# Layer 1: values projected once a pixel and moved to the patch positions by transfers within SBUF

## The chip, the cores and the metric

The kernel runs on one core of a Trainium2 chip. The metric is the device time of one execution in microseconds. Three runs of the kernel before gave 4286.24, 4290.92 and 4291.43 us; the median is 4290.92.

The engines are named as in the profile: PE (TensorE: matrix products; PEld is its loading of the stationary operand, which overlaps), DVE (VectorE), ACT (ScalarE), POOL (GpSimd), and SP (SyncE), which computes nothing and issues DMAs. SBUF is the working memory of 128 partitions, PSUM the memory that PE writes.

## The reference

The network has four layers, numbered 0 to 3, on images of 56 x 56 pixels with 192 channels, 8 in the batch, all in float32; each layer adds its result to its input after a group norm. The change is in layer 1, the second one, an attention over 3 x 3 patches with stride 2:

```python
v = x @ Wv
vp = jnp.pad(v, ((0, 0), (PAD, PAD), (PAD, PAD), (0, 0)))
patches = jnp.stack([vp[:, i:i + STRIDE * h:STRIDE, j:j + STRIDE * w:STRIDE, :] for i in range(K) for j in range(K)], axis=3)
patches = patches.reshape(Bn, h * w, KK, HEADS, HEAD_DIM)
pooled = x.reshape(Bn, h, STRIDE, w, STRIDE, C).mean(axis=(2, 4))
a = pooled.reshape(Bn, h * w, C) @ Wa + ba
a = a.reshape(Bn, h * w, HEADS, KK, KK) * SCALE
a = jax.nn.softmax(a, axis=-1)
out = jnp.einsum('bnhpq,bnqhd->bnphd', a, patches)
...
for i in range(K):
    for j in range(K):
        acc = acc.at[:, i:i + STRIDE * h:STRIDE, j:j + STRIDE * w:STRIDE, :].add(out[:, :, :, idx, :])
        idx += 1
...
return y @ Wp + bp
```

There are 28 x 28 positions an image and 9 places in each patch (K is 3, KK is 9), so a pixel stands in 9/4 patches in the mean. The value of a pixel, `x @ Wv`, doesn't depend on the patch in which it stands. There are 6 heads of 32 channels.

## The kernel before, in words

Layer 1 works on units, `(p, t)`: a pair of images p (4 of them) and a strip t of 8 image rows (7 of them), 28 units in all. Channels lie on partitions: parts j = 0 and 1 hold the first 128 channels of the two images, part 2 the other 64 channels of both, one image on partitions 0 to 63, the other on 64 to 127 (`sides`).

For unit n the steps are:

- `load(n)` issues 6 DMAs for the strip (L788).
- `normalize(n)` has ACT scale and shift the strip into `xn` (L834), where rows stand in pairs and each has a column of zeros ahead of it (57 columns, `W1`). One more pair of rows at the top holds the row above the strip, copied from the unit before or cleared (L829, L831). POOL adds 2 x 2 pixels into `pool` (L839, L841).
- `patches(n)` copies `xn` nine times, once for each place q in the patch, into `xc`, so that for each position the nine pixels stand side by side: five copies on DVE, two on POOL (q 3 and 7), two on ACT (q 1 and 5) (L856 to L860).
- `values` multiplies `xc` by `Wv`. A step takes one row of 28 positions, as two groups of 14 positions x 9 places = 126 pixels, for two images: eight matmuls (L924, L930), with the pixels stationary and the 192 columns of `Wv` moving, and one eviction on ACT (L934). There are four steps in a unit. The result, `v`, has (q, position) on 126 partitions.
- `attention` has two parts. `logits` multiplies `pool` by `Wa` (L875, L879), adds the bias and subtracts the largest (DVE, POOL). `weights` takes the exponential (ACT), sums and inverts (DVE), scales (POOL, L895) and stores the result to DRAM as `ad` (L900).
- `spread` brings `ad` back into `bd` with 14 DMAs (L913), in such a layout that the matrix `bd` of a group has its attention weights in the right columns and zeros elsewhere. There are two `bd` buffers.
- `attend` multiplies `v` by `bd` (L959): 96 matmuls, 8 groups of 12, whose sums in PSUM are at once the weighted sum and the adding back to the image. It evicts to `ys` and carries the row that two strips share.
- `fold` multiplies `ys` by `Wp` (L1002 to L1013) and adds the result to the strip (L1025). `finish` stores it with 6 DMAs (L984) and takes statistics for the next layer's norm.

The loop over units n (L1064) is a pipeline written out by hand. In one turn it loads unit n + 4, normalizes n + 3, makes the patches of n + 2, attends n, multiplies the logits of n + 2, makes the values of n + 1 (with the weights of n + 2 after the second step), spreads n + 2 and folds n. Ahead of the loop units 0 and 1 are brought to the same state.

The order of PE, DVE, ACT and POOL is the program's (`manual_schedule` at L770). SP is not in that list: the order of its DMAs is set by the framework's planner when the program is built. [...]

Most DMAs of the kernel, and all of layer 1's loop, are issued on SP. Two buffers `c` in PSUM serve logits, values and fold in turn.

Of the kernel before, what the change touches and what calls it, by code (L numbers as in the profile page):

```python
# [10 lines left out]
ALU = mybir.AluOpType  # L11
# [4 lines left out]
C = 192  # L16
CP = 96
H = 56
# [712 lines left out]
def layer1(cx, xin, xout, w, consts):  # L731
# [27 lines left out]
    with ExitStack() as es:  # L759
# [55 lines left out]
        nc.sync.dma_start(bp, w["bp"])  # L815

        xns = [cx.tile(cp, [128, NR + 1, 3, 2, W1], f"xn{i}") for i in range(2)]


        bds = [cx.tile(cp, [NP, 2 * NG, NCOL, HEADS, 3], f"bd{i}") for i in range(2)]
# [1 line left out]
        def normalize(n):  # L824

            p, t = units[n]
            x, xn = xs[n], xns[n % 2]
            if t == 0:
                nc.gpsimd.memset(xn[:, 0, :, 1, :], 0.0)  # L829
            else:  # L830
                nc.gpsimd.tensor_copy(xn[:, 0, :, 1, :], xns[(n - 1) % 2][:, NR, :, 1, :])  # L831
            for j in range(3):
                s, o = norms[p][:, j, 0:1], norms[p][:, j, 1:2]
                nc.scalar.activation(  # L834
                    xn[:, 1:, j, :, 1:], x[:, j].rearrange("p (y i x) -> p y i x", i=2, x=H),
                    AF.Identity, bias=o, scale=s,
                )
            rows = cx.tile(sp, [128, NR, 3, H], "rows")
            nc.gpsimd.tensor_tensor(rows, xn[:, 1:, :, 0, 1:], xn[:, 1:, :, 1, 1:], ALU.add)  # L839
            pool4 = cx.tile(wk, [128, 3, NR, N], "pool")  # L840
            nc.gpsimd.tensor_tensor(  # L841
                pool4.rearrange("p j y x -> p y j x"), rows[:, :, :, 0:H:2], rows[:, :, :, 1:H:2], ALU.add
            )
            return pool4.rearrange("p j y x -> p j (y x)")

        def patches(n):

            xn = xns[n % 2]
            xc = cx.tile(wk, [128, 3 * NR, 2, KK, NX], "xc")
            for q in range(KK):  # L850
                j, i = divmod(q, 3)
                src = xn[:, (i + 1) // 2 : (i + 1) // 2 + NR, :, (i + 1) % 2, j : j + 2 * N - 1 : 2]
                src = src.rearrange("p y j (u x) -> p (y j) u x", u=2)
                dst = xc[:, :, :, q, :]
                if q in (3, 7):
                    nc.gpsimd.tensor_copy(dst, src)  # L856
                elif q in (1, 5):
                    nc.scalar.copy(dst, src)
                else:
                    nc.vector.tensor_copy(dst, src)  # L860
            return xc

        def attention(pool4, out):

# [47 lines left out]
                at = 2 * x * 3 * HEADS  # L912
                nc.sync.dma_start(bd[x : x + (KK - 1) * NX + 1 : NX, :, at : at + HK], av[x])  # L913

        def values(xc, v):


            def step(r):
                pv = cx.tile(psc, [128, 2, 512], "c")
                out = lambda i, u: pv[0:NP, i, u * C : (u + 1) * C]  # L920
                group = lambda j, u: xc[:, 3 * r + j, u].rearrange("p q x -> p (q x)")
                for u in range(2):
                    for i in range(2):
                        nc.tensor.matmul(  # L924
                            out(i, u), group(i, u), wv[0], start=(u == 0), stop=True,
                            skip_group_check=True,
                        )
                for u in range(2):
                    for i in range(2):
                        nc.tensor.matmul(  # L930
                            out(i, u), group(2, u)[sides[i]], wv[1][sides[i]], start=False, stop=True,
                            skip_group_check=True,
                        )
                nc.scalar.copy(  # L934
                    v[:, :, 2 * r : 2 * r + 2, :].rearrange("p i g c -> p i (g c)"),
                    pv[0:NP, :, 0 : 2 * C],
                )

            return [lambda r=r: step(r) for r in range(NR)]


        blocks = [[(0, h) for h in range(4)], [(1, h) for h in range(4)]]
# [3 lines left out]
        def attend(n, v):  # L946
# [4 lines left out]
            for g in range(NG):  # L951
                r, half = divmod(g, 2)
                i0 = int(t == 0 and r == 0)
                c0 = int(half == 0)
                dims = (NCOL - c0, 3 - i0)
                to = (half * 2 * NX + c0 - 1) * NY + 2 * r + i0
                for k, block in enumerate(blocks):
                    for u, (i, h) in enumerate(block):
                        nc.tensor.matmul(  # L959
                            sub(py[u * HD : (u + 1) * HD, k, to:], (NY, dims[0]), (1, dims[1])),  # L960
                            v[:, i, g, h * HD : (h + 1) * HD],
                            bd[:, i * NG + g, c0:, h, i0:],
                            start=(g == 0), stop=True, skip_group_check=True,
                        )
# [68 lines left out]
        def clear(n):  # L1033
            (nc.gpsimd, nc.vector)[n].memset(bds[n], 0.0)

        vs, xcs, pools = {}, {}, {}
        for i, xn in enumerate(xns):
            nc.gpsimd.memset(xn[:, :, :, :, 0], 0.0)
        pools[0] = normalize(0)
        xcs[0] = patches(0)  # L1040
# [3 lines left out]
        first[0]()  # L1044
        pools[1] = normalize(1)
        clear(0)
        vs[0] = cx.tile(wk, [NP, 2, NG, C], "v")
        todo = values(xcs.pop(0), vs[0])
        todo.pop(0)()
        todo.pop(0)()  # L1050
        first[1]()
        spread(0, ads.pop())
        for f in todo:
            f()
        second = attention(pools.pop(1), ads)
        second[0]()
        clear(1)
        second[1]()
        spread(1, ads.pop())
        xcs[1] = patches(1)  # L1060
        pools[2] = normalize(2)
        for p in range(1, NPAIR - 1):
            fetch_norms(p, nc.sync)
        for n in range(len(units)):  # L1064
            if n == 2:
                for f in cx.late:
                    f(lambda: cx.tile(psb, [128, 512], "b"))
                fetch_norms(NPAIR - 1, nc.sync)
            load(n + 4)
            if n + 3 < len(units):  # L1070
                pools[n + 3] = normalize(n + 3)
            if n + 2 < len(units):
                xcs[n + 2] = patches(n + 2)
            ys = attend(n, vs.pop(n))
            if n + 1 < len(units):
                vs[n + 1] = cx.tile(wk, [NP, 2, NG, C], "v")
                todo = values(xcs.pop(n + 1), vs[n + 1])
                if n + 2 < len(units):
                    logits, weights = attention(pools.pop(n + 2), ads)
                    logits()  # L1080
                    todo.insert(2, weights)
                for f in todo:
                    f()
                if ads:
                    spread(n + 2, ads.pop())
            if late and late[0][0] <= n:
                late.pop(0)[1]()
            fold(n, ys)
# [950 lines left out]
```

## Time and profile before

| what | us |
|---|---|
| median of three runs | 4290.92 |
| the profiled execution | 4297.32 |
| its span, first to last instruction | 4295.5 |
| PE busy in the span | 4052.9 |
| DVE, ACT, POOL busy | 2340.9, 1781.9, 1510.6 |
| `attend` (L959), start of the first and the last matmul | 2150.6, 2753.5 |

The profile is one execution, taken by the hardware profiler. A row of a group names line, engine, operation, what is written and read, the number of instructions and their times. A row of a DMA issue (SPq) gives the time that the issue took on SP, not that of the transfer. "Busy" leaves DMA issues out. In a timeline, neighbouring instructions of one line are merged; its columns are start, duration, engine, line, operation and number. In the chain of waits, which is followed back from the last instruction, each piece is what the next one waited for. A window's columns are explained where one is shown. Some of PE's records are missing, so their numbers can be a few per cent low; each float32 matmul leaves two records.

### The profile page before, as it was taken

The numbers are of one execution on the slowest core, as the hardware profiler recorded it, in microseconds if no ns is written. First come the engines' busy times: TensorE is split into PE (matmuls) and PEld (weight loads), VectorE is DVE, ScalarE is ACT, GpSimd is POOL, SyncE is SP. The second block draws the span as 40 slices with busy tenths as digits, with TensorE's granted clock in tenths as the row PEclk, the third lists the DMA queues.
The fourth block names the chain that finished last, engine by engine and source line by source line (L and its number), as shares of the span: only waits on it lengthen the run. The fifth ranks groups of instructions, "written<-read, shape, count | busy, mean of one in ns | idle before, by whom it ended". The sixth has DMA issues, their size and how long they took to land.

```text
span 4295.5 us, 106533 instructions
## 1 busy us (share of the span) xinstructions
PE 4052.9 (94%) x46380; PEld 2655.7 (62%) x46380; DVE 2340.9 (54%) x3429; ACT 1781.9 (41%) x2052; POOL 1510.6 (35%) x1295
## 2 busy tenths in 40 slices
PE   6999999999999999999699999769998999998997
PEld 4666767676676767667366666524444555555997
DVE  4446565554656545554444444366665666664664
ACT  2334434334443333443233344223334555554664
POOL 3223232222322222232133333133334444444776
PEclk9999999999999999999899999889999999999999
DMA  6755242242524224241224344455547676664243
GB/s 137 143 106 144 61 114 62 78 96 61 143 62 111 56 74 109 61 109 59 80 72 109 96 107 105 121 173 171 165 140 180 171 174 156 155 152 114 71 117 93
DMA packets 379607, 484.14 MB, mean 113 GB/s; under 512 B 175780, under 2 KB 324372, under 8 KB 377236
## 3 DMA queue, kind: packets, MB, share of 16 engines
q1 hardware_dynamic: 373636, 466.97, 42.8%
q10 hardware_dynamic: 5504, 10.35, 0.8%
q8 instruction: 365, 5.98, 0.6%
q14 instruction: 102, 0.84, 0.1%
HBM read 321.49 MB, written 155.65 MB: 111 GB/s over the span
## 4 chain that ended last, share of the span: by engine, by line
PE 79%; DVE 6%; issue 5%; SPq 3%; DMA 3%; ACT 2%; POOL 1%; DVEq 0%; ACTq 0%; POOLq 0%
PE c L294 10%; PE c L376 6%; PE v L1371 6%; PE c L301 5%; PE c L462 4%; PE c L417 4%; PE c L924 4%; PE h L1873 4%; PE c L352 4%; PE y L959 3%; PE kv L1431 3%; PE c L442 3%; PE c L424 3%; DVE ol L359 2%; PE c L1583 2%
## 5 line engine op out<-in xcount | busy, mean ns | idle before, releaser
L325 POOL TENSOR_TENSOR qv<-s,s 128x392 f32<-128x392 f32 (+3 forms) x320 | 568.5, 1798 | 1453.5 <-ACT s L310 1453.0
L310 ACT ACTIVATE s<-c,bqv 128x784 f32<-128x784 f32 (+1 forms) x320 | 278.2, 910 | 383.9 <-PE c L301 189.1
L294 PE MATMUL c<-xa,wqv 128*128 128x392 f32 x1152 | 433.2, 518 | 4.3 <-DVE xa L49 2.7
L359 ACT COPY or<-c 56x1024 f32<-56x1024 f32 (+1 forms) x288 | 256.2, 901 | 424.4 <-DVE ol L359 414.5
L319 DVE TENSOR_TENSOR qv<-s,s 128x784 f32<-128x784 f32 (+1 forms) x160 | 205.8, 1287 | 265.0 <-ACT s L310 265.0
L359 DVE COPY ol<-c 56x1024 f32<-56x1024 f32 (+1 forms) x288 | 299.8, 1076 | 39.8 <-PE c L352 38.5
L294 PEld LDWEIGHTS c<-xa,wqv 128*128 128x128 f32 x1152 | 211.1, 194 | 176.8 <-issue 39.3
L376 PEld LDWEIGHTS c<-or,ol 120*64 120x64 f32 x9216 | 275.8, 139 | 39.5 <-issue 29.6
L376 PE MATMUL c<-or,ol 120*64 120x56 f32 x9216 | 284.5, 223 | 11.5 <-DMA ol<-ed 7.7
L352 PEld LDWEIGHTS c<-ident,qv 64*120 64x120 f32 x4032 | 256.1, 138 | 55.1 <-issue 35.6
L352 PE MATMUL c<-ident,qv 64*120 64x64 f32 x4032 | 282.8, 224 | 3.6 <-POOL qv L325 2.5
L1371 PE MATMUL v<-wvb,wa 128*128 128x512 f32 (+1 forms) x400 | 192.1, 612 | 50.5 <-ACT wa L1282 31.3
L301 PE MATMUL c<-xb,wqv 64*128 64x392 f32 x1152 | 232.9, 518 | 0.0
L431 ACT ACTIVATE s<-c,bp 128x448 f32<-128x448 f32 x224 | 129.7, 630 | 248.7 <-PE c L424 248.6
L1904 POOL TENSOR_TENSOR y<-y,s 128x448 f32<-128x448 f32 x168 | 185.0, 1101 | 92.7 <-ACT s L1883 92.7
L1873 PE MATMUL h<-ringv,am 128*64 128x57 f32 (+1 forms) x4400 | 192.7, 235 | 19.6 <-DVE ringv L1860 11.8
L462 PE MATMUL c<-po,wo 128*128 128x448 f32 x448 | 198.1, 564 | 7.0 <-DVE po L451 7.0
L1873 PE MATMUL h<-ringh,am 128*64 128x57 f32 (+1 forms) x4400 | 186.3, 232 | 7.8 <-DVE ringh L1879 7.8
L1382 ACT ACTIVATE vb<-sm 128x1024 f32<-128x1024 f32 (+1 forms) x100 | 103.7, 1038 | 212.2 <-issue 187.2
L417 PE MATMUL c<-xa,wp 128*128 128x224 f32 x896 | 191.1, 356 | 0.0
L405 DVE TENSOR_TENSOR acca<-c,acca 128x392 f32<-128x392 f32 (+1 forms) x120 | 67.3, 587 | 219.2 <-PE c L467 204.8
L1873 PEld LDWEIGHTS h<-ringv,am 128*64 128x64 f32 x4400 | 168.1, 140 | 22.9 <-DVE ringv L1860 12.7
(221 smaller groups left out, 7591.9 us busy)
## 6 DMA issues: line engine op xcount, KB each, us to landing
or<-tt SPq DMA_DIRECT2D x252, 196.0 KB
ol<-tt SPq DMA_DIRECT2D x252, 196.0 KB
vt<-v SPq DMA_DIRECT2D x56, 672.0 KB
v<-vb SPq DMA_DIRECT2D x96, 384.0 KB
x<-x SPq DMA_DIRECT2D x112, 168.0 KB
x<-x SPq DMA_DIRECT2D x112, 112.0 KB
bt<-bs SPq DMA_DIRECT2D x28, 448.0 KB
bs<-bs SPq DMA_DIRECT2D x56, 224.0 KB
```

What stands on the lines that cost most here:

```text
L294: nc.tensor.matmul(ps[:, h, 0:n], wqv[0][:, j, :], xn[0][:, at : at + n], start=True, stop=False,)
L301: nc.tensor.matmul(ps[:, h, 0:n], wqv[1][rows, j, :], xn[1][rows, g * n : (g + 1) * n], start=False, stop=True,)
L310: nc.scalar.activation(t, ps[rows, :, 0:n], AF.Silu, bias=bqv[rows, j : j + 1])
L319: nc.vector.tensor_tensor(sub(qv[rows, 7 * g :, 64 + H - 1 :], (HH * 120, 2), (120, 7), (-1, H)), *(t.rearrange("p u (h w) -> p u h w", w= ...
L325: eng.tensor_tensor(sub(qv[rows, w0:, H - 1 - 7 * g - HH * u :], (120, w1 - w0), (-1, 7)), *(t[:, u].rearrange("p (h w) -> p w h", w=H)[:, ...
L352: nc.tensor.transpose(view(i // 8)[:, :, i % 8], qv[e : e + DS, i0 + i, :], ident[e : e + DS, e : e + DS],)
L359: copy(dst, src[rows])
L376: nc.tensor.matmul(ps[u * 64 : (u + 1) * 64, k, v * H : (v + 1) * H], left[:, d * H : d * H + 64], right[:, d * H : (d + 1) * H], start=Tr ...
L417: nc.tensor.matmul(out(u, h), wp[0][:, 2 * j + u, :], xn[0][:, at : at + n], start=(u == 0), stop=True, skip_group_check=True,)
L462: nc.tensor.matmul(pa, wo[:, 2 * j + u, 0:CA], pos[u], start=(u == 0), stop=(u == 1))
L1371: nc.tensor.matmul(out, x[:, at : at + n], wt, start=(k == 0), stop=(k == 1), skip_group_check=True,)
L1873: nc.tensor.matmul(ps[sides[c], y], am[a][:, m * CB : (m + 1) * CB], old[:, x], start=(n < 2), stop=True, skip_group_check=True,)
```

## The change

- There is no `patches` and no `xc`. `xn` loses its extra pair of rows.
- `values(n)` multiplies each pixel of the strip once. A step takes two pairs of rows, 2 x 57 = 114 pixels each, for two images: eight matmuls as before, with 114 pixels stationary where there were 126. Two steps make a unit, each with one eviction on ACT. The result `vp` has (row of the pair, column) on 114 partitions and five pairs of rows; the first pair is the last one of the strip above, copied by POOL, or cleared at t = 0.
- `gather(n)` moves `vp` to `v`: for each of the nine places q and each half u of a row of positions, one DMA from every second of 27 partitions of `vp` to 14 partitions of `v`. Each is 14 x 4 x 384 numbers, in pieces of 1536 B: 18 DMAs a unit, 504 in all, on SP.
- There are three `v` buffers, not two, and the index of the image is now inside that of the group.
- In the loop, the values are made for unit n + 2, not n + 1, with the weights after the first step; then come the gather and the spread of n + 2.

```diff
-        xns = [cx.tile(cp, [128, NR + 1, 3, 2, W1], f"xn{i}") for i in range(2)]
+        xns = [cx.tile(cp, [128, NR, 3, 2, W1], f"xn{i}") for i in range(2)]
...
-            if t == 0:
-                nc.gpsimd.memset(xn[:, 0, :, 1, :], 0.0)
-            else:
-                nc.gpsimd.tensor_copy(xn[:, 0, :, 1, :], xns[(n - 1) % 2][:, NR, :, 1, :])
...
-        def patches(n):
-
-            xn = xns[n % 2]
-            xc = cx.tile(wk, [128, 3 * NR, 2, KK, NX], "xc")
-            for q in range(KK):
-                j, i = divmod(q, 3)
-                src = xn[:, (i + 1) // 2 : (i + 1) // 2 + NR, :, (i + 1) % 2, j : j + 2 * N - 1 : 2]
...
-        def values(xc, v):
+        def values(n):
+
+
+            xn = xns[n % 2]
+            vp = vps[n] = cx.tile(wk, [2 * W1, NR + 1, 2, C], "vp")
+            above = vps.pop(n - 1, None)
+            if units[n][1] == 0:
+                nc.gpsimd.memset(vp[:, 0], 0.0)
+            else:
+                nc.gpsimd.tensor_copy(vp[:, 0], above[:, NR])
...
-            def step(r):
+            def step(k):
                 pv = cx.tile(psc, [128, 2, 512], "c")
-                out = lambda i, u: pv[0:NP, i, u * C : (u + 1) * C]
-                group = lambda j, u: xc[:, 3 * r + j, u].rearrange("p q x -> p (q x)")
+                out = lambda i, u: pv[0 : 2 * W1, i, u * C : (u + 1) * C]
+                pixels = lambda j, u: xn[:, 2 * k + u, j].rearrange("p a x -> p (a x)")
...
-            return [lambda r=r: step(r) for r in range(NR)]
+            return [lambda k=k: step(k) for k in range(NR // 2)]
+
+        def gather(n):
+
+            rows = vs[n % NV].rearrange("p (r u) i c -> p u r (i c)", u=2)
+            for q in range(KK):
+                j, i = divmod(q, 3)
+                for u in range(2):
+                    at = (i + 1) % 2 * W1 + u * 2 * NX + j
+                    src = vps[n][at : at + 2 * NX - 1 : 2].rearrange("p r i c -> p r (i c)")
+                    r = int(i > 0)
+                    nc.sync.dma_start(rows[q * NX : (q + 1) * NX, u], src[:, r : r + NR])
...
+        NV = 3
+        vs = [cx.tile(cp, [NP, NG, 2, C], f"v{k}") for k in range(NV)]
+        vps, pools = {}, {}
...
+            ys = attend(n, vs[n % NV])
             if n + 2 < len(units):
-                xcs[n + 2] = patches(n + 2)
-            ys = attend(n, vs.pop(n))
-            if n + 1 < len(units):
-                vs[n + 1] = cx.tile(wk, [NP, 2, NG, C], "v")
-                todo = values(xcs.pop(n + 1), vs[n + 1])
-                if n + 2 < len(units):
-                    logits, weights = attention(pools.pop(n + 2), ads)
-                    logits()
-                    todo.insert(2, weights)
+                todo = values(n + 2)
+                logits, weights = attention(pools.pop(n + 2), ads)
+                logits()
+                todo.insert(1, weights)
                 for f in todo:
                     f()
-                if ads:
-                    spread(n + 2, ads.pop())
+                gather(n + 2)
+                spread(n + 2, ads.pop())
```

More of the change, by code (lines that the diff above doesn't have):

```diff
@@ L834, in normalize @@
                 nc.scalar.activation(
-                    xn[:, 1:, j, :, 1:], x[:, j].rearrange("p (y i x) -> p y i x", i=2, x=H),
+                    xn[:, :, j, :, 1:], x[:, j].rearrange("p (y i x) -> p y i x", i=2, x=H),
                     AF.Identity, bias=o, scale=s,
@@ L838, in normalize @@
             rows = cx.tile(sp, [128, NR, 3, H], "rows")
-            nc.gpsimd.tensor_tensor(rows, xn[:, 1:, :, 0, 1:], xn[:, 1:, :, 1, 1:], ALU.add)
+            nc.gpsimd.tensor_tensor(rows, xn[:, :, :, 0, 1:], xn[:, :, :, 1, 1:], ALU.add)
             pool4 = cx.tile(wk, [128, 3, NR, N], "pool")
@@ L844, in normalize @@
             return pool4.rearrange("p j y x -> p j (y x)")
-        def patches(n):
-            xn = xns[n % 2]
-            xc = cx.tile(wk, [128, 3 * NR, 2, KK, NX], "xc")
-            for q in range(KK):
-                j, i = divmod(q, 3)
-                src = xn[:, (i + 1) // 2 : (i + 1) // 2 + NR, :, (i + 1) % 2, j : j + 2 * N - 1 : 2]
[L853 to L861, printed above, removed]
         def attention(pool4, out):
@@ L924, in step @@
                         nc.tensor.matmul(
-                            out(i, u), group(i, u), wv[0], start=(u == 0), stop=True,
+                            out(i, u), pixels(i, u), wv[0], start=(u == 0), stop=True,
                             skip_group_check=True,
@@ L930, in step @@
                         nc.tensor.matmul(
-                            out(i, u), group(2, u)[sides[i]], wv[1][sides[i]], start=False, stop=True,
+                            out(i, u), pixels(2, u)[sides[i]], wv[1][sides[i]], start=False, stop=True,
                             skip_group_check=True,
@@ L934, in step @@
                 nc.scalar.copy(
-                    v[:, :, 2 * r : 2 * r + 2, :].rearrange("p i g c -> p i (g c)"),
-                    pv[0:NP, :, 0 : 2 * C],
-                )
-            return [lambda r=r: step(r) for r in range(NR)]
+                    vp[:, 2 * k + 1 : 2 * k + 3].rearrange("p u i c -> p i u c"),
+                    pv[0 : 2 * W1, :, 0 : 2 * C].rearrange("p i (u c) -> p i u c", c=C),
+                )
+            return [lambda k=k: step(k) for k in range(NR // 2)]
[8 more added lines that the diff above has]
+                    nc.sync.dma_start(rows[q * NX : (q + 1) * NX, u], src[:, r : r + NR])
         blocks = [[(0, h) for h in range(4)], [(1, h) for h in range(4)]]
@@ L960, in attend @@
                             sub(py[u * HD : (u + 1) * HD, k, to:], (NY, dims[0]), (1, dims[1])),
-                            v[:, i, g, h * HD : (h + 1) * HD],
+                            v[:, g, i, h * HD : (h + 1) * HD],
                             bd[:, i * NG + g, c0:, h, i0:],
@@ L1034, in clear @@
             (nc.gpsimd, nc.vector)[n].memset(bds[n], 0.0)
-        vs, xcs, pools = {}, {}, {}
+        NV = 3
+        vs = [cx.tile(cp, [NP, NG, 2, C], f"v{k}") for k in range(NV)]
+        vps, pools = {}, {}
         for i, xn in enumerate(xns):
@@ L1039, in layer1 @@
         pools[0] = normalize(0)
-        xcs[0] = patches(0)
         nc.gpsimd.tensor_scalar(ba, ba, 4.0, None, ALU.mult)
@@ L1044, in layer1 @@
         first[0]()
+        for f in values(0):
+            f()
+        gather(0)
         pools[1] = normalize(1)
         clear(0)
[L1047 to L1050, printed above, removed]
         first[1]()
         spread(0, ads.pop())
-        for f in todo:
-            f()
         second = attention(pools.pop(1), ads)
         second[0]()
+        for f in values(1):
+            f()
+        gather(1)
         clear(1)
@@ L1059, in layer1 @@
         spread(1, ads.pop())
-        xcs[1] = patches(1)
         pools[2] = normalize(2)
```

## The prediction

> **What bounds the kernel now.** The page's slices give PE nines almost throughout, an average over four layers; the change lives in layer 1, where the tile view of `y` puts `attend` (L959) from 2150.6 to 2753.5 us. I then read, for that stretch: busy time by windows, the chain of waits, SP's timeline, the rows of DMA issues.
>
> Windows (start:end, length, then busy us and count of PE, PE's weight loads, DVE, ACT, POOL; granted clock, DMA share, GB/s); the second is one unit:
>
> ```profile
> 2201.00:2708.00 507.00, 501.09 (x6518) 338.18 (x6518) 218.31 (x388) 201.83 (x263) 181.21 (x225) 0.99 0.41 102
> 2269.10:2290.20 21.10, 21.10 (x282) 14.14 (x280) 9.22 (x16) 8.54 (x11) 7.93 (x10) 1.00 0.42 108
> ```
>
> PE never rests; DVE, ACT and POOL work under 45% of the unit. The copies that the change deletes are therefore not what sets the pace. The chain through that unit (start, us, line):
>
> ```profile
> 2269.15 4.49 PE y L959 x166
> 2273.63 1.81 PE c L875 x4
> 2275.45 1.00 PE c L879 x4
> 2276.45 1.50 PE c L924 x8
> 2277.95 0.85 PE c L930 x8
> ...
> 2285.83 1.70 PE c L1002 x4
> 2287.53 0.95 PE c L1004 x4
> 2288.48 0.90 PE b L1008 x4
> 2289.39 0.90 PE b L1013 x4
> 2290.29 4.48 PE y L959 x167
> ```
>
> A unit is attend 4.5, logits 2.8, values 9.4 (2276.45 to 2285.83: four steps of 1.50 + 0.85), fold 4.45: 21.1 us. Over all units it is 22.2: (2753.5 - 4.5 - 2150.6) / 27.
>
> SP, the queue that issues the DMAs, over nearly the same unit:
>
> ```profile
> 2266.02 0.32 SPq L900 DMA_DIRECT2D ad<-aq  x1
> 2267.76 0.30 SPq L984 DMA_DIRECT2D x<-x  x1
> 2268.29 3.02 SPq L788 DMA_DIRECT2D x<-x  x6
> 2271.41 10.89 SPq L913 DMA_DIRECT2D bd<-ad  x14
> 2282.34 3.64 SPq L984 DMA_DIRECT2D x<-x  x5
> 2287.16 0.32 SPq L900 DMA_DIRECT2D ad<-aq  x1
> ```
>
> The lines add up to 18.2 us of the 21.1 between the two `ad` stores, and to 17.2 in the next unit (stores 2.73). I take 17.7. So a second engine stands close behind PE, with some 3.5 us left, and the page's table of busy time, which counts no DMA issues, doesn't show it.
>
> [...] `bd<-ad` has 724 ns at least and 725 in the median over 392 issues, too even for a wait on data. [...] SP issues for 17.7 us a unit, the DMA engines move for 0.42 x 21.1 = 8.9. [...]
>
> **The change part by part, a unit.**
>
> 1. Values, four steps to two. Each keeps its eight matmuls of 192 moving columns; the stationary side goes from 126 to 114 pixels[...]. PE: -2 x 2.35 = -4.7, so 16.4 us of work. ACT loses two evictions of 0.80.
> 2. No patches: DVE -5 copies, ACT -2, POOL -2 and the carried row of `xn` (0.33). POOL gains the copy or clearing of `vp`'s first row, 114x384: between 0.33 (128x171) and 0.52 (128x336). All on engines with over half the unit free, so 0; on a full POOL the copy would cost its 0.5. The copy waits for `above` (ACT, a unit earlier) and for the gather two units back; POOL's softmax subtraction queues behind it. Both are long done in any order I can make.
> 3. Gather: 18 DMAs a unit on SP, each 14 partitions x 4 pieces of 1536 B. They wait for `values(n + 2)`, which PE does in unit n; behind them on SP are the spread of the attention weights, stores and loads. Nothing takes DMAs off SP, and all of a unit's 45 must pass through it in order, so SP's unit becomes 17.7 + 18 x (x + 0.05), x the time of one issue and 0.05 what lies between two (10.89 / 14 - 0.725).
>
> x has no row of its own; the nearest:
>
> ```profile
> L275 SPq DMA_DIRECT2D or<-tt x252: 69/326/1714, 267.9 to 2019.0; - x126
> L275 SPq DMA_DIRECT2D ol<-tt x252: 306/386/3244, 269.3 to 2019.3; - x126
> L913 SPq DMA_DIRECT2D bd<-ad x392: 724/725/1488, 2137.9 to 2741.7; - x196
> L1447 SPq DMA_DIRECT2D bias<-in_l_rel_bias x64: 620/621/726, 2809.8 to 2854.5; - x64
> L1391 SPq DMA_DIRECT2D v<-vb x96: 359/461/1403, 2859.2 to 3248.7; - x96
> L1496 SPq DMA_DIRECT2D vt<-v x56: 584/616/1366, 3260.8 to 3861.2; - x56
> ```
>
> (min/median/max ns). `or`/`ol` have one piece a partition, 56 partitions: 0.31 is the floor. `v<-vb` and `vt<-v` have two and seven pieces a partition, `bias` and `bd` few outer elements (8 and 9), as the gather has (14). I take 0.57, amid the rows with several pieces: 18 x 0.62 = 11.2, SP's unit 28.9. Ends: 0.31 gives 24.2; 0.725 gives 31.7.
>
> 4. Does the data fit? Queue q1 of the page moves 466.97 MB in 373,636 packets at 42.8% of 16 engines: 0.428 x 16 x 4295.5 us for it, 15.9 B/ns an engine. A gather unit is 18 x 86,016 B = 1.55 MB, 6.1 us over 16 engines[...]. It doesn't bind; it can delay an issue, which the upper end covers.
>
> 5. Does SP ever wait? With three `v` and two `bd` buffers, unit n+2's gather and spread wait for `attend(n - 1)` and `attend(n)`. PE's work of a unit takes 16.4, so in a unit of 28.9 it is done before SP's next `ad` store needs the softmax weights. SP runs without gaps and PE waits for `bd`: `attend` is late next, released by a DMA.
>
> **Sum.** The 26 units that issue for a later one: 26 x (28.9 - 22.2) = +174. At the start, gather 0 falls into the time before the first spread (2137.9), when SP is mostly idle; gather 1 puts 11 us ahead of spread 1, which had some 6 to spare (last issue about 2164, needed 2172.9): +5. At the end, attend 27 follows the last spread at once instead of 7 us later: -4. Together +175. The profiled execution took 4297.3 (span 4295.5); 4297.3 + 175 = 4472. The runs' median is 6.4 lower, so 4466.
>
> **Rivals.**
> - Cheap issue (x 0.30 to 0.45, as `or`/`ol`): SP still binds, less. At 0.386: 17.7 + 7.8 = 25.5, +3.3 x 26 = +86: 4378; at the floor of 0.31, 4343. [...] Against: one piece a partition only.
> - Dear issue (over 0.75): `bias` to `bd` is +104 ns from 8 outer elements to 9. If that slope held to 14, x = 1.24, the unit 40.9 and the time 4291 + 26 x 18.7 = 4778. Against: the same rows differ also in pieces (8 and 144), and `or`/`ol` show no such slope.
> - Faster: SP absorbs the gathers. It decides where 17.7 + 18 (x + 0.05) is below 22.2, at x under 0.20. Then up to 4.5 a unit is gained, down to SP's own 17.7 (PE's 16.4 lies below it): 4291 - 117 = 4174. For it: one `or<-tt` in 252 took 69 ns, and part of SP's 17.7 may be stalls that shrink. Against: the lowest median of any DMA issue is 0.257 us (L235, one piece of 448 B, twice).
> - No change to tell (within 0.2%, 8.6 us, about what a measurement can tell here): x within 0.02 of 0.20. A coincidence.
> - Not as described: were the eight matmuls a step slower for reading `xn` in place, PE would have to lose 12 us a unit to matter under SP's 28.9. Their operands are contiguous runs of 114; left out.
>
> **How the numbers follow.** Forecast (x 0.45 to 0.75) 0.60, its own range 4410 to 4550; cheap 0.20; dear 0.12; faster 0.06; same 0.02. Low end 4345 takes in nearly all of the cheap case; high end 4575 takes 0.725 with 40 us for stalls behind busier DMA engines, and leaves the dear case out. Faster 0.06, same 0.02, slower 0.92.
>
> **What would show it.** In the changed profile: values with half the records in L924's and L930's successors and a step still near 2.35 us (step 1); a group of 504 `v<-vp` issues whose median is x (step 3); SP's timeline without gaps from the first spread to the last; PE idle before `attend`, released by `bd<-ad` or `v<-vp`, some 12 us a unit (step 5)[...]. It is wrong if SP shows gaps while PE stays full, if x is under 0.30, or if the wait before `attend` follows the landing of transfers long since issued, which would put the DMA engines in SP's place.

## The result, and the profile after

The changed kernel takes 4648.92 us in the median of four runs (4644.17 to 4655.16), the kernel before on the same chip 4291.18 (4286.24 to 4297.21). The ratio is 1.0834, interval 1.0812 to 1.0856. It is slower, as forecast, but by 358 us where 175 had been worked out, and outside the range. The profiled execution took 4644.4 us (span 4642.6), 347.1 more than that of before.

First the page's slices, 116 us each, in tenths (PE's busy share, the granted clock, the share of the DMA engines), and the chain of work that ended last, by engine and line:

```profile
PE   6999999999999999995455545546999899999997
...
PEclk9999999999999999997778777777999999999999
DMA  6644251524332332314444444445453876664243
...
PE 61%; SPq 20%; DVE 6%; issue 6%; DMA 4%; ACT 2%; POOL 2%; ACTq 0%; DVEq 0%; POOLq 0%
PE c L294 9%; SPq L936 8%; SPq L891 6%; PE c L376 6%; PE v L1365 6%; PE c L301 5%; PE c L462 4%; PE c L417 4%; PE h L1867 3%; PE c L352 3%; PE kv L1425 3%; PE c L442 2%; PE c L424 2%; PE c L467 2%; DVE ol L359 2%
```

The nines of PE now have a hole of ten slices. It is layer 1. In the chain, the gather's issues (L936) and those of the spread (L891) hold 14% of the span by themselves: issues on SP, not transfers and not matmuls.

The tile views of `vp` and of `y` (minimum/median/maximum in ns, first and last start in us):

```profile
L936 SPq DMA_DIRECT2D v<-vp x504: 807/807/1884, 2122.7 to 3086.3; - x168
L920 ACT COPY vp<-c x56: 779/792/800, 2119.5 to 3051.9; 114x768 f32<-114x768 f32 x56
L902 POOL COPY vp<-vp x24: 502/507/510, 2140.3 to 3046.0; 114x384 f32<-114x384 f32 x24
```

```profile
L956 PE MATMUL y<-bd,v x5376: 246/341/350, 2155.6 to 3105.6; 126*32 126x84 f32 x96, 126*32 126x87 f32 x96, 126*32 126x56 f32 x4, 126*32 126x58 f32 x4
```

The number that the forecast had to guess is in the first row: an issue of the gather takes 0.807 us. The first start of `attend` is 5.0 us later than before, and the mean distance of two is (3105.6 - 6.0 - 2155.6) / 27 = 35.0 us (6.0 for the last one's own length), where it was 22.2. Those 27 distances hold 345.6 of the 347.1 us.

SP's timeline over one unit:

```profile
2440.42 0.53 SPq L878 DMA_DIRECT2D ad<-aq  x1
2441.05 15.51 SPq L936 DMA_DIRECT2D v<-vp  x18
2456.66 10.76 SPq L891 DMA_DIRECT2D bd<-ad  x14
2467.52 3.08 SPq L788 DMA_DIRECT2D x<-x  x6
2470.70 0.52 SPq L878 DMA_DIRECT2D ad<-aq  x1
```

Each line begins 0.1 us after the one above ends. The view of SP's waits over 800 us of the stretch (total, times, longest) says the same:

```profile
SPq L788 <- DMA x<-x: 7.6, 11, 1.9
SPq L795 <- DMA norm<-nn: 2.2, 1, 2.2
SPq L891 <- PE b L1010: 0.7, 1, 0.7
```

Summed over SP's records of 17 units (2403.9 to 2998.9 us), a unit of 35.0 us holds 32.5 us of issues (gathers 15.0, spread 10.1, stores 3.1, loads 3.1, the rest 1.1, of which 0.4 are short waiting instructions ahead of some issues) and 2.25 of the pauses of about 0.05 between them. SP is full. PE beside it, over the same unit, in its timeline:

```profile
2442.96 0.91 PE L916 MATMUL c<-wv,xn 64*114 64x192 f32 x8
2446.09 1.77 PE L999 MATMUL c<-ys,wp 128*128 128x448 f32 x4 [2.22 <-POOL ys L967]
...
2449.64 0.97 PE L1010 MATMUL b<-ys,wp 64*64 64x448 f32 x4
2469.46 5.96 PE L956 MATMUL y<-bd,v 126*32 126x84 f32 x192 [18.85 <-DMA bd<-ad]
```

All of a unit but `attend` is done by 2450.6. Then PE stands 18.85 us until the last `bd` has landed, which SP had issued at 2467.4. The window over the stretch (columns as in the prediction):

```profile
2200.00:3000.00 800.00, 415.20 (x5543) 272.35 (x5541) 187.89 (x280) 139.55 (x164) 158.06 (x172) 0.77 0.42 106
```

PE works 52% of the time, the DMA engines 42%, DVE, ACT and POOL less than a quarter. Nothing in this stretch is full but the queue that the table of busy times leaves out.

### The profile page after: what moved, and what is told of

Its sections match the earlier page's. It is cut to its first block, busy times and chain, and to the rows that moved or that the text cites. A ratio compares the mean times of both kernels' runs of the same rounds, so it can differ in the third digit from the quotient of the medians.

```text
span 4642.6 us, 105099 instructions
## 1 busy us (share of the span) xinstructions
PE 3962.9 (85%) x45484; PEld 2586.0 (56%) x45484; DVE 2294.5 (49%) x3289; ACT 1712.7 (37%) x1940; POOL 1488.5 (32%) x1239
## 4 chain that ended last, share of the span: by engine, by line
PE 61%; SPq 20%; DVE 6%; issue 6%; DMA 4%; ACT 2%; POOL 2%; ACTq 0%; DVEq 0%; POOLq 0%
PE c L294 9%; SPq L936 8%; SPq L891 6%; PE c L376 6%; PE v L1365 6%; PE c L301 5%; PE c L462 4%; PE c L417 4%; PE h L1867 3%; PE c L352 3%; PE kv L1425 3%; PE c L442 2%; PE c L424 2%; PE c L467 2%; DVE ol L359 2%
## 5 line engine op out<-in xcount | busy, mean ns | idle before, releaser
L956 PE MATMUL y<-bd,v 126*32 126x84 f32 (+3 forms) x5376 | 171.2, 310 | 428.4 <-DMA bd<-ad 286.0
L956 PEld LDWEIGHTS y<-bd,v 126*32 126x32 f32 x5376 | 164.3, 150 | 450.2 <-issue 353.9
L862 DVE TENSOR_TENSOR s<-c,ba 112x972 f32<-112x972 f32 x28 | 32.8, 1171 | 554.3 <-PE c L857 490.3
L829 ACT ACTIVATE xn<-x,norm 128x448 f32<-128x448 f32 x84 | 61.5, 760 | 625.1 <-DMA x<-x 624.6
L834 POOL TENSOR_TENSOR rows<-xn 128x672 f32<-128x672 f32 x28 | 38.7, 1384 | 606.6 <-ACT xn L829 588.3
```

The costliest lines, as they stand in the source:

```text
L956: nc.tensor.matmul(sub(py[u * HD : (u + 1) * HD, k, to:], (NY, dims[0]), (1, dims[1])), v[:, g, i, h * HD : (h + 1) * HD], bd[:, i * NG + ...
```

## The experiments

All of them start from the changed kernel. Medians are of four runs, ratios stand against the kernel before run beside them.

| run | us | ratio and interval | unit, us |
|---|---|---|---|
| one_piece | 4630.52 | 1.0780 (1.0751 to 1.0810) | 34.5 |
| tiny | 4652.18 | 1.0829 (1.0802 to 1.0856) | 35.2 |
| half_gather | 4446.96 | 1.0355 (1.0332 to 1.0378) | 27.6 |
| half_pool | 4482.55 | 1.0457 (1.0431 to 1.0483) | 28.5 |
| no_gather | 4267.21 | 0.9932 (0.9909 to 0.9954) | 21.1 |
| half_act | 4644.19 | 1.0815 (1.0792 to 1.0839) | 34.3 |
| act_all | 4575.75 | 1.0673 (1.0646 to 1.0700) | 31.4 |
| pool_all | 4408.48 | 1.0280 (1.0254 to 1.0307) | 25.6 |
| pool_all_dve | 4418.67 | 1.0285 (1.0258 to 1.0311) | 25.9 |
| late_norm | 4498.86 | 1.0477 (1.0449 to 1.0504) | 28.9 |
| late_norm_act | 4510.36 | 1.0506 (1.0480 to 1.0532) | 29.4 |
| mid_norm | 4411.37 | 1.0260 (1.0243 to 1.0277) | 25.7 |
| via_dram | 4641.95 | 1.0810 (1.0790 to 1.0830) | 34.4 |
| via_dram_pool | 4641.15 | 1.0807 (1.0788 to 1.0825) | 34.6 |
| via_dram_pool2 | 4772.02 | 1.1112 (1.1092 to 1.1131) | 39.3 |

The unit is the mean distance of two `attend`s, from the records of their first matmuls. `shapes` and `shapes_apart` were executed once each; only issue times are read from them.

### What sets the cost of one issue: shapes, one_piece, shapes_apart

The theory after the result was that the gather's four pieces a partition make its issue dear. `shapes` puts a battery of DMAs on SP ahead of layer 0, back to back (`a` and `b` lie in SBUF, `h` in DRAM; the first index is the partition, and 4 of the second are four rows of 1536 B):

```diff
+        for k in range(4):
...
+            nc.sync.dma_start(b[0:14, 0:8:2], a[0:28:2, 0:4])
+            nc.sync.dma_start(b[14:28, 0:4], a[0:14, 0:4])
...
+            nc.sync.dma_start(b[42:56, 0:1], a[0:14, 0:1])
+            nc.sync.dma_start(b[56:72, 0:8:2], a[0:16, 0:4])
...
+            nc.sync.dma_start(c[60:74, 0:8:2], h[0:14, 0:4])
...
```

> The changed kernel with a set of extra transfers ahead of layer 0, each shape on a line of its own, four times each: 8, 9, 11, 12, 14, 16, 28, 32, 56, 64 and 112 partitions, in four pieces of 1536 B a partition or in one contiguous run, from SBUF or from DRAM. They compute nothing and add some 60 us at the start. What is read is the median issue time by line. If the number of pieces sets the issue's cost, the shapes with one contiguous run a partition take 0.31 to 0.39 us and those with four take 0.7 to 0.85, whatever the number of partitions. If the short outermost dimension sets it, 8 to 14 partitions take 0.6 to 0.85 with one run or with four, and 16, 28, 32 and more take 0.3 to 0.5. If having both ends in SBUF, or stepping over every second partition, sets it, the transfers from DRAM or with a step of one stand apart from the others.

Fourteen partitions took 0.82 us with four pieces, 0.81 with one run of 6144 B and 0.79 with one of 1536 B; 16 partitions took 0.65 and 0.60. Whether a partition has one piece or four hardly matters, nor does the number of bytes. Nor is there a slope with the number of partitions: 8, 9, 11, 12, 14, 28 and 56 lay between 0.74 and 0.85. The battery is crowded, though, and in the last three of its four rounds some rows can't be read as costs of their own: the gather's exact shape, first in each round, took 2.4 to 2.5 us, 14 partitions in four pieces out of DRAM 0.83 to 1.59, and 32, 64 and 112 partitions within SBUF 0.67 to 0.93, 0.89 to 1.10 and 1.38 to 1.54. The same question on the kernel itself: `one_piece` lays `v` so that each gather writes one run of 6144 B a partition.

```diff
-            rows = vs[n % NV].rearrange("p (r u) i c -> p u r (i c)", u=2)
+            rows = vs[n % NV].rearrange("p (u r) i c -> p u (r i c)", u=2)
...
-                            v[:, g, i, h * HD : (h + 1) * HD],
+                            v[:, half * NR + r, i, h * HD : (h + 1) * HD],
```

> The changed kernel with v laid out so that each gather writes one contiguous run of 6144 B a partition, where it wrote four of 1536 B; same number of gathers, same bytes. If the pieces set the cost of an issue: its median falls from 0.807 to 0.31 to 0.39, SP's unit from 35.0 to about 27, and the time to about 4435. If the short outermost dimension (14) sets it: the median stays within 0.05 of 0.807 and the time within 30 us of 4649.

Its tile view of `vp`:

```profile
L936 SPq DMA_DIRECT2D v<-vp x504: 107/746/2134, 2122.9 to 3072.6; - x168
```

Four times fewer pieces took 0.061 us off an issue, 18 us off the time. The pieces theory falls. Left were the wait behind other transfers and the two memories. `shapes_apart` lets each DMA of the battery wait until the one before has landed, and adds the same shapes out of DRAM.

> The changed kernel with extra transfers ahead of layer 0, as in the first set of shapes, but all to the same place, so that each waits for the one before to land and nothing is queued when it is issued; four times each. They compute nothing and add some 150 us. If the gather's 0.807 us is its own cost, 14 partitions within SBUF stay at 0.75 to 0.85 in four pieces and in one; if it is made by what is queued ahead of it, they fall to 0.3 to 0.4. If the source counts, 14 partitions from DRAM lie 0.2 or more under the same from SBUF[...].

Issue times in us, from the trace's records, the last three of four rounds:

| partitions, pieces | SBUF to SBUF | DRAM to SBUF |
|---|---|---|
| 9, one | | 0.26 |
| 14, four | 0.90 to 0.91 | 0.33 to 0.34 |
| 14, one | 0.81 to 0.85 | 0.31 to 0.32 |
| 16, four | 0.66 to 0.70 | 0.32 to 0.33 |
| 16, one | 0.57 to 0.61 | |
| 56, four | 0.87 to 0.89 | |
| 56, one | | 0.31 |
| 64, one | | 0.48 to 0.51 |
| 112, four | 0.66 to 0.69 | |
| 112, one | | 0.31 |
| 128, one | 0.51 to 0.53 | |

So the cost is the issue's own, with nothing in flight ahead of it. It goes with both ends being SBUF: every number of partitions measured both ways costs at least twice what it costs out of DRAM, the gather's shape 2.7 times. Why is open. Within SBUF, 14 and 56 partitions cost some 0.2 more than 16, 112 and 128; out of DRAM there is no such step between them, but 64 partitions stand apart there, unexplained. And one piece against four says nothing of more: `bd<-ad`, nine partitions out of DRAM as well, has 16 pieces a partition and takes 0.725 in the loop, where one piece takes 0.26 here. Of the crowded rows of `shapes`, 32 and 64 partitions took 0.67 to 1.10, so the grouping is a pattern of five shapes and not a cause that was shown.

### Is it the issue time that bounds? tiny, half_gather, no_gather, half_pool

`tiny` keeps all 18 issues with their partitions, pieces and waits and moves 64 B in place of each 1536. `half_gather` issues the nine of u = 0 alone, `no_gather` none. In all three, what isn't moved of `v` stays zero.

```diff
-                    nc.sync.dma_start(rows[q * NX : (q + 1) * NX, u], src[:, r : r + NR])
+                    nc.sync.dma_start(
+                        rows[q * NX : (q + 1) * NX, u, :, 0:16], src[:, r : r + NR, 0:16]
+                    )
```

> The 18 gathers keep their place, partitions, four pieces and waits, but each piece is 64 B instead of 1536 B: v is zero but for the first 16 of its 384 columns, so the output is not the reference's, and about 1.5 MB a unit of data is gone. Theory (SP's time to issue is the bound, and its cost has nothing to do with the bytes): v<-vp at 0.78 to 0.85 us, SP with hardly a gap, unit 33.5 to 35 us, time 4600 to 4650. Rival (the landing of the data, as via_dram made one think): as without gathers, 4270 to 4350.

> Only the nine gathers of the first half of a row pair are issued (v of the other half stays zero, so the output is not the reference's). Theory (each issue is worth its SP time): SP unit 19.2 + 9 x (0.84 + 0.05) = 27.2 us, time 4650 - 26 x 7.8 = 4445 (4415 to 4485), near half_pool's 4482 where all the data moves. Rival (the bound lies elsewhere and gives way only when the gathers are gone, or at once): 4550 or more, or under 4350.

> The changed kernel without the gathers: v is cleared once and stays zero, so layer 1 adds nothing but its bias term; all matmuls are still made. If the gathers' issue time is the whole loss: SP's unit falls from 35.0 to about 19.2, PE's is 16.4, and the time to about 4649 - 26 x 15.8 = 4240, under the kernel before by some 50, with SP and not PE as what sets the unit. If SP's other DMAs weren't close behind, PE would set it: 26 x 5.8 under the kernel before, about 4140.

`tiny`, its tile view of `vp`, a window, and SP's waits in that window:

```profile
L936 SPq DMA_DIRECT2D v<-vp x504: 807/807/2111, 2115.8 to 3087.5; - x168
```

```profile
2300.00:2900.00 600.00, 307.18 (x4148) 200.92 (x4148) 140.54 (x204) 102.05 (x120) 115.26 (x125) 0.76 0.26 65
```

```profile
SPq L788 <- DMA x<-x: 9.2, 13, 1.6
```

The DMA share falls from 0.42 to 0.26, and the time stays: 1.0829 against 1.0834. The data moved is worth nothing here; the 18 issues are worth everything. `half_gather`, the same window:

```profile
2300.00:2900.00 600.00, 397.47 (x5304) 258.75 (x5300) 180.12 (x262) 131.25 (x153) 147.49 (x162) 0.84 0.42 107
```

It came to 4447 where the sum over SP said 4445: nine issues fewer took 202 us off the time and 7.4 us off the unit, 0.82 for each, which is 0.84 and the pause of 0.05 less a little. SP's issues and short pauses filled 594 of these 600 us.

`no_gather` shows the bottom:

```profile
2300.00:2700.00 400.00, 336.56 (x4756) 214.14 (x4757) 156.68 (x226) 114.72 (x134) 130.97 (x144) 0.93 0.43 106
```

Without any gather the kernel is only 0.7% faster than before. SP's issues and pauses still fill 378 of these 400 us. So PE's shorter unit could not be had in full even with gathers at no cost: what comes next, most likely SP's other 27 issues, leaves 1.1 us under the old unit of 22.2.

`half_pool` moves all the data and lets POOL issue the half with u = 1.

```diff
-                    nc.sync.dma_start(rows[q * NX : (q + 1) * NX, u], src[:, r : r + NR])
+                    (nc.sync, nc.gpsimd)[u].dma_start(rows[q * NX : (q + 1) * NX, u], src[:, r : r + NR])
```

> The changed kernel with nine of the eighteen gathers a unit issued by POOL. Moving nine to ACT left the time where it was: there SP's next issues waited for ACT's transfers that had used the same completion semaphore. If SP's issue time sets the unit and POOL's transfers have semaphores of their own: SP's unit falls to about 27 us, the time to about 4450. If the transfers themselves set it, whoever issues them: 4640, as before.

```profile
L936 SPq DMA_DIRECT2D v<-vp x252: 807/807/1807, 2118.0 to 2909.8; - x126
L936 POOL DMA_DIRECT2D v<-vp x252: 545/545/763, 2118.6 to 2902.4; - x126
```

166 us of the 358 are gone, with the same transfers. It stays 36 us above `half_gather`; SP had 28 us of pauses over 0.15 us in 400 us here.

### Can another engine issue them? half_act, act_all, pool_all and four variants

`half_act` is `half_pool` with ACT, 17% busy in the changed kernel's stretch, in POOL's place.

> The changed kernel with the gathers of one half (u = 1) issued by ACT, nine of eighteen a unit. If SP's issue time sets the unit: SP's falls by 9 x 0.85 = 7.7 to 27.3 us, which 26 units turn into about -200: 4450; ACT, some 6 us busy a unit, has room for 7.7 more. If the transfers themselves (the DMA engines) set the unit, the time stays near 4649.

SP's timeline, ACT's beside it, and SP's waits over 2300 to 2700 us:

```profile
2449.27 7.83 SPq L936 DMA_DIRECT2D v<-vp  x9
2457.21 16.85 SPq L891 DMA_DIRECT2D bd<-ad  x14
```

```profile
2458.51 8.10 ACTq L936 DMA_DIRECT2D v<-vp  x9
```

```profile
SPq L891 <- DMA v<-vp: 75.8, 14, 8.1
```

SP saved 7.7 us on the gathers and lost 6 on the spread. An issue of `bd` itself still took 0.725 us; between them SP stood until a gather had landed, most likely one of ACT's: with all 18 on SP, the view of the changed kernel's waits has none for a gather. What the two queues share shows in the trace of the changed kernel: the 3296 issues of SP and the 41 of ACT name the same eight semaphores (counters that engines wait on) for their landing, the next one in turn in 3258 of 3336 steps, and 2297 of SP's wait for the one that they name. ACT's gathers began at 2458.51, behind its copy of `vp` (2457.70, 0.78 us), when SP had been at the spread since 2457.21; a wait took 5.4 us in the mean.

`act_all` puts all 18 on ACT.

> The changed kernel with all eighteen gathers issued by ACT: SP is left with 20 us a unit, ACT has 6 + 18 x 0.87 = 22. If shared completion semaphores hold SP behind ACT's transfers, SP's issues of the weights wait for the gathers as in the half version and the time stays between 4500 and 4650, with idle time on SP put down to v<-vp. If they don't, ACT sets a unit of about 22 and the time is near 4300.

Its waits, over the same 400 us:

```profile
ACT xn L829 <- DMA v<-vp: 156.9, 7, 24.6
...
PE c L999 <- POOL ys L967: 117.5, 10, 15.4
```

Now normalize stands behind the gathers on ACT, and what needs it comes late. 73 us better than the changed kernel, no more.

`pool_all` puts all 18 on POOL. None of SP's seven longest waits in `half_pool` (12.4 us to 1.7 in 400) was for `v<-vp`.

> The changed kernel with all eighteen gathers issued by POOL. SP is then left with some 20 us a unit, as in the kernel without gathers (4267). POOL has 7 us of work a unit and 18 issues of a cost that no row shows. If SP's issue time was the bound, the unit is the larger of 20 and 7 + 18 y: at y = 0.7 about 4270, at 1.0 about 4380, at 1.5 about 4610. If the transfers set it: 4640, with POOL not full.

```profile
2300.00:2700.00 400.00, 292.40 (x3779) 177.04 (x3780) 126.18 (x181) 98.61 (x116) 256.67 (x391) 0.86 0.79 145
...
PE c L999 <- POOL ys L967: 68.6, 12, 9.8
POOL v L936 <- DMA v<-vp: 57.1, 73, 2.3
```

At the 0.545 us that an issue took on POOL the expectation came to 4270 or less; it missed. With `mid_norm` below, which is level with it, this is the best that moves all the data, 4408, still 2.8% over before. SP is no longer full to the last us (334 of 400 in issues and short pauses), and two things are new: fold waits for the carry's addition, which stands behind gathers on POOL, and the DMA share is 0.79. POOL's own queue has 34.8% of the 16 engines in this window, 8.9 us a unit; on SP's queue the same gathers took 0.42 x 35.0 - 0.43 x 21.1 = 5.6 us, by the windows of the changed kernel and of `no_gather`. Part of that may be crowding: SP's queue rose as well, from 8.8 us a unit in `no_gather` (41.8%) to 11.0 (43.1%). But in `half_pool`, at a share of 0.57, POOL's nine already took 14.7%, 4.2 us a unit, against 2.8 for half of SP's 5.6.

Three tries at the orders around it followed: `pool_all_dve` gives the carry and the row above to DVE; `late_norm` puts normalize after the spread as well; `mid_norm` puts it between the values and the gather. The edit to the carry, and `mid_norm`'s to the order:

```diff
-                nc.gpsimd.tensor_tensor(ys[:, :, 0, :], ys[:, :, 0, :], carry.pop(0), ALU.add)
+                nc.vector.tensor_tensor(ys[:, :, 0, :], ys[:, :, 0, :], carry.pop(0), ALU.add)
```

```diff
-            if n + 3 < len(units):
-                pools[n + 3] = normalize(n + 3)
             ys = attend(n, vs[n % NV])
...
+                if n + 3 < len(units):
+                    pools[n + 3] = normalize(n + 3)
                 gather(n + 2)
```

> As pool_all (18 gathers straight within SBUF, all on POOL), with the carry's add and copy and the copy of the row above put on DVE. If what keeps pool_all at 25.8 us a unit is fold waiting for the carry's add behind POOL's gathers (10 us a wait was seen): unit 21.5 to 23.5 us, time 4290 to 4350. If it is the gathers' landing itself (v late, DMA share .79): 4390 to 4410, as pool_all, with PE waiting for DMA v<-vp instead.

> pool_all_dve with normalize of unit n + 3 put after the gather and spread of unit n + 2 instead of ahead of attend. In pool_all_dve ACT's evictions of the values stood behind normalize's, which waited for x to land 9 us after its issue (PE c L910 waited 8.6 to 9.9 us for ACT vp). If that is what is left: unit 22 to 24 us, 4300 to 4360. If the landing of x is late whatever waits for it (DMA share .80): 4390 to 4420.

> late_norm with normalize of unit n + 3 one step earlier: after the values of unit n + 2 and ahead of its gather. In late_norm the two POOL additions of normalize stood behind the 18 gathers on POOL and PE c L853 waited 9.6 to 11 us for them; ACT's evictions of the values no longer waited for normalize. If both waits go: unit 22 to 24 us, 4300 to 4370, below pool_all_dve's 4419. If the wait for x only moves from ACT to the logits of the next unit, or x lands late whatever waits: 4390 to 4440.

None of the gains came: two times lay outside both of their ranges, and `mid_norm`'s in its second one. In `pool_all_dve` the wait of fold went, and PE waited as long for ACT's evictions of the values, behind a normalize that waited for its strip. In `late_norm` that went too, but the two POOL additions of normalize came to stand behind the 18 gathers, which I had not priced (waits over 2300 to 2900 us):

```profile
PE c L853 <- POOL pool L836: 191.1, 20, 11.1
```

`mid_norm` mended that and was back at 4411, with PE waiting ahead of `attend` again, the DMA share at 0.80. Three orders (`pool_all`, `pool_all_dve`, `mid_norm`) came out within 11 us of each other with three different waits, which suggests that something beside the order on ACT and POOL holds them. `late_norm_act`, `late_norm` with the stores of x issued by ACT, gave 4510.

```diff
-                nc.sync.dma_start(xout[d][at], src)
+                nc.scalar.dma_start(xout[d][at], src)
```

> late_norm with the six stores of x of a unit issued by ACT: SP falls by some 3.1 us a unit. If SP is still what paces late_norm: another 20 to 80 us off, 4250 to 4330, perhaps level with the kernel before. If SP and ACT wait for each other's transfers through the semaphores that they share, as in half_act: within 20 us of late_norm, or slower.

Taking 3 us a unit of issues off SP changed nothing for the better, and SP had paused for 109 of 400 us in `late_norm`, so its issue time doesn't pace that one. What does pace the versions on POOL, the landing of transfers at a share of 0.80 or SP's waits for them (some 78 us of pauses over 0.15 us in 400 us of `mid_norm`), was not separated.

### A cheaper road for the data: via_dram, via_dram_pool, via_dram_pool2

If an issue is cheap with DRAM at one end, `vp` can be stored to DRAM and fetched from there, nine DMAs in place of 18, after the spread, into a `v` laid out as in `one_piece`.

```diff
+            nc.sync.dma_start(
+                vd.rearrange("w r i c -> w (r i c)"), vps[n].rearrange("w r i c -> w (r i c)")
+            )
...
+                src = bass.AP(
+                    vd.tensor, vd.offset + at * long + int(i > 0) * 2 * C,
+                    [[2 * long, NX], [2 * NX * long, 2], [1, NR * 2 * C]],
+                )
+                to = vs[n % NV][q * NX : (q + 1) * NX].rearrange("p (u r) i c -> p u (r i c)", u=2)
+                nc.sync.dma_start(to, src)
```

> vp is stored once a unit to a DRAM tile (1 issue), and nine DMAs, still on SP, bring it back to v after the unit's 14 spread issues (one for each patch position, both halves together, 6144-byte runs). The number of bytes into v is the same; store and loads have DRAM on one side. Theory (the cost of an issue is set by the kind of its source: 0.81 us where it is SBUF with 14 partitions, about 0.33 from DRAM): v<-vd at 0.30 to 0.42 us of SP each, SP unit 19.2 + 0.6 + 9 x 0.40 = 23.4 us, time near 4650 - 26 x 11.6 = 4350 (4310 to 4410). Rival (an issue in this loop costs about 0.8 us whatever it moves, so only the count matters): 19.2 + 10 x 0.85 = 27.7 us, time near 4460. Rival (the wait for the store to land holds SP): a gap of over 1 us on SP ahead of the first v<-vd, and a time over 4400.

Its tile view of `vd`:

```profile
L947 SPq DMA_DIRECT2D v<-vd x252: 307/385/1282, 2133.9 to 3081.9; - x126
L930 SPq DMA_DIRECT2D vd<-vp x28: 263/264/327, 2126.7 to 3063.5; - x28
```

The issues cost what the theory said, 0.385 and 0.264, and the time did not move: 4642. SP's timeline and its waits over 2300 to 2900 us:

```profile
2513.57 10.87 SPq L891 DMA_DIRECT2D bd<-ad  x14
2524.48 4.19 SPq L947 DMA_DIRECT2D v<-vd  x9
2529.70 7.93 SPq L991 DMA_DIRECT2D x<-x  x6
```

```profile
SPq L991 <- DMA v<-vd: 97.4, 90, 2.9
```

The nine loads are issued in 4.2 us, but each brings 172 KB, and the stores of x behind them wait for their landing, 1.08 us each in the mean of the 90 waits, so the six hold SP for 7.93 us. Over the same 600 us SP had, in a unit of 34.4 us, 23.2 us of issues, 1.4 of short pauses and 9.7 of longer ones, where the changed kernel had 0.3. The share of the DMA engines rose to 0.63. One bound went and the next stood at almost the same place.

`via_dram_pool` gives the nine loads to POOL, `via_dram_pool2` the six loads of x as well.

> As via_dram, with the nine v<-vd loads issued by POOL. Theory (SP's issue time is the bound): SP is left with 19.2 + 0.6 = 19.8 us a unit, and the unit goes to 20.5 to 22 us as in the run without gathers (21.4): time near 4290 (4250 to 4340). POOL pays 9 x 0.55 = 5 us a unit. Rival (data: store and loads put about 2.4 MB a unit on the DMA engines): DMA share over 0.85 and a unit above 23 us, 4340 or more.

> As via_dram_pool, with the six x loads of a unit on POOL too. Theory: SP falls to about 16.7 us a unit, about what PE has to do (16.4), and the unit to 18 to 20 us: time near 4220 (4190 to 4270), below the kernel before. Rival: POOL (15 issues of 0.55 us = 8.2 us plus its own work of about 7 us, some of it behind waits for transfers) or the DMA engines become the bound: no faster than via_dram_pool, 4260 or more, PE waiting for POOL ys or for DMA v<-vd.

Both missed. Their waits over 2300 to 2900 us, in that order:

```profile
POOL v L947 <- DMA vd<-vp: 341.6, 17, 24.9
```

```profile
ACT s L867 <- POOL s L864: 396.4, 15, 29.3
PE c L1009 <- POOL ys L977: 291.4, 13, 25.3
...
POOL x L788 <- DMA x<-x: 211.0, 12, 20.3
```

In `via_dram_pool` POOL stood 20.1 us in the mean of 17 waits for the store of `vp`, and over the same 600 us ACT waited 212.0 us for POOL's part of the softmax and PE 124.6 for the carry. In `via_dram_pool2` POOL stood 17.6 us in the mean of 12 waits for an earlier DMA of x, and those two waits came to 396.4 and 291.4 us. No run that moves all the data beat the kernel before; the one time below it is `no_gather`'s, which moves none of it.

## Why the prediction was right or wrong

**Direction and mechanism: right.** The steps that failed are sizes: above all step 3's x, then SP's other issues and the start. Step 5 said that SP runs without gaps and PE waits for `bd` ahead of `attend`. The profile shows it (34.7 of 35.0 us, the wait of 18.85 us), and `tiny` and `half_gather` show the bound to be issue time: the first took 23 of 24 bytes away and kept the time, the second took half the issues and came within 2 us of its sum.

**Step 3, the term of x: mis-sized, and most of the error.** x was taken as 0.57; it measured 0.807 in the median and 0.837 in the mean of the 17 units, so 18 x 0.267 = 4.8 us a unit. It even lay over the upper end of 0.725. The choice was made "amid the rows with several pieces"; `shapes` and `one_piece` showed that four pieces cost hardly more than one, and `shapes_apart` that the two memories count. All six rows that the price was taken from have DRAM at one end, and that was the unknown to bound. The profile of before has one issue with SBUF at both ends, in the same view as the row of `bias`:

```profile
L1448 SPq DMA_DIRECT2D bias<-bias x1: 551/551/551, 2856.3 to 2856.3; - x1
```

It has 64 partitions. By itself it would have confirmed 0.57: the same memories aren't enough, as the number of partitions counts too (within SBUF 14 took some 0.2 more than 16). The rival of the dear issue had the right sign and its point of decision (0.75) was passed, but its reason fell: `shapes` has 0.74 for 8 partitions and 0.83 for 9, but no further rise up to 14, and 1.24 us was never near.

**SP's other issues: mis-sized.** "I take 17.7" came from two units, by adding the lengths of timeline lines, without the pauses between lines. Summed over the issue records of the kernel before from 2201 to 2708 us, a unit had 17.5 us of issues and 1.4 of short pauses, 18.9. The changed kernel has 34.72 - 15.07 - 0.9 = 18.75 beside the gathers. That is 1.05 a unit. With it and 0.28 of remaining waits, 4.8 + 1.05 + 0.28 gives 6.1, the difference of 35.0 and 28.9.

**The start: mis-sized, with a figure that fits by chance.** The forecast of +5 was for `attend` 1, which needed its weights at 2172.9 and had some 6 us to spare. That `attend` began at 2186.05, 13.1 late. The first `attend` was 5.0 late, which the prediction didn't foresee. SP in the changed kernel:

```profile
2142.16 0.83 SPq L936 DMA_DIRECT2D v<-vp  x1
2143.09 10.78 SPq L891 DMA_DIRECT2D bd<-ad  x14
2153.91 16.02 SPq L936 DMA_DIRECT2D v<-vp  x17
...
2173.32 10.86 SPq L891 DMA_DIRECT2D bd<-ad  x14
```

One gather of unit 1 stood ahead of spread 0 and waited until 2142.16 for its values (spread 0 began at 2137.90 before); the other seventeen took 16.0 us ahead of spread 1, not 11.

**The sum.** The 26 distances from `attend` 1 to `attend` 27 are 35.15 us in the mean, 6.25 over the forecast's 28.9: some 163 of the 172 us between 4472 and the profiled 4644.4. The start adds 8. The end came as said: (3100.0 - 2749.2) - 347.1 = 3.7 us saved after the last `attend` began, against 4. By terms, x is 26 x 4.8 = 125 of the 172, SP's other issues 26 x 1.05 = 27, its remaining waits 26 x 0.28 = 7.

**Step 1: right in kind.** Two steps of values start 2.3 us apart, as before. PE was busy 0.52 x 35.0 = 18.2 us a unit, not 16.4, at a granted clock of 0.77 in the stretch, where the window of before had 0.99. It cost nothing, as PE is not what is late.

**Step 2: right.** The copy of `vp`'s first row took 0.507 us on POOL, within its bounds, on an engine 20% busy.

**Step 4: right.** The data doesn't bind, as `tiny` shows. The forecast's 6.1 and 8.9 make 15.0 us a unit, a share of 0.52 of its 28.9; the share was 0.42, 14.7 us of the longer unit.

**The other rivals.** Cheap issue: 0.31 to 0.34 is the price out of DRAM, not within SBUF. Faster: `no_gather` gives its floor as 4267, not 4174; most likely SP's own work, 378 of 400 us there, kept the unit from going lower. The chances rested on x, and the case beyond 0.75 had been given 0.12 on an argument about one slope.

## What to carry to other kernels

Price a DMA's issue from a row with the same memories at both ends and about the same number of partitions; where there is none, that is the unknown to bound: here six rows between other memories said 0.33 to 0.73, one between the same memories, but with other partitions, 0.551, and the gather took 0.807. When a queue is near full, add up all its issues and the pauses between them over many units: two units read from merged lines were 1.2 us short here. Before an issue is moved to another queue, look at what stands behind it there and for whose landings it waits: on ACT, normalize waited 156.9 us in 400 for the gathers' landing (`act_all`); with half of them there, SP's spread waited 75.8 (`half_act`). Most of the ways tried here to move this gather gave back most of the gain to such waits.

## What was not expected of the hardware

- Issued alone, a DMA within SBUF took 0.51 to 0.91 us on SP, one out of DRAM 0.26 to 0.34 (0.48 to 0.51 with 64 partitions); the store of `vp` to DRAM took 0.264. Within SBUF 14 and 56 partitions cost some 0.2 more than 16, 112 or 128.
- 24 times fewer bytes left an issue of the gather at 0.807 us (`tiny`).
- POOL issued the same DMA in 0.545 us (`pool_all`), ACT in 0.832 (`act_all`).
- In four runs the granted clock was lower where PE was busy for less of the time: 0.99 at 99% busy (before), 0.93 at 84% (`no_gather`), 0.84 at 66% (`half_gather`), 0.77 at 52% (the change), where `attend` took 5.96 us against 4.49.
- Gathers of POOL's queue held the DMA engines 8.9 us a unit (`pool_all`), those of SP's 5.6, for the same bytes, perhaps in part by crowding; nine of them in `half_pool` took 4.2.
- Moving nine issues to ACT made SP wait 75.8 us in 400 for landings of gathers (`half_act`); in the changed kernel's trace the issues of both, 3296 and 41, name the same eight semaphores.
